# A conditioned fp32 block: the second entry's feed-forward weight in halves, its leaf sums on VectorE, and new places for late sums, last leaf sums and last stores

## The chip, the cores and the metric

The kernel runs on one core of one Trainium2 chip. The metric is the device time of one execution in microseconds. Five engines work side by side on the core: TensorE (PE, with its weight loads PEld), VectorE (DVE), ScalarE (ACT), GpSimd (POOL) and SyncE (SP, which issues most DMAs here; ACT issues some as well). Each engine runs its instructions in the order in which the program gives them; only semaphores tie engines together.

## The reference, cut to what matters

Input `x` has 2 batch entries of 2048 rows of 512 floats; `cond` has one row for each entry. All is fp32.

```python
emb = silu(t) @ ada_w + ada_b            # six rows of 512 for each entry
shift_msa, scale_msa, gate_msa, shift_mlp, scale_mlp, gate_mlp = split(emb, 6)
norm  = ln(x) * (1 + scale_msa) + shift_msa
h     = gelu(norm @ ssm_w1 + ssm_b1)               # 512 -> 512, exact gelu
x     = x + gate_msa * (h @ ssm_w2 + ssm_b2)       # 512 -> 512
norm2 = ln(x) * (1 + scale_mlp) + shift_mlp
hf    = gelu_tanh(norm2 @ ff_w1 + ff_b1)           # 512 -> 1024
x     = x + gate_mlp * (hf @ ff_w2 + ff_b2)        # 1024 -> 512
```

## The kernel before, in words

**Blocks.** The 4096 rows are cut into 8 blocks of 512 rows. Blocks 0 to 3 belong to the first entry, blocks 4 to 7 to the second. Each block goes through four stages, named in the trace by their tiles: `hA` (first hidden layer), `oA` (its residual), `hC` (feed-forward hidden layer), `oC` (feed-forward residual). A hand-written order interleaves the blocks: turn `i` of the main loop runs `hC` of block i, `oA` of block i+1, `oC` of block i, and `hA` of block i+2. TensorE goes through these stages without a break where it can.

**Fewer multiplications by sums.** No matrix product is done directly. `hA` and `oA` use seven half-size products (P1 to P7, in the order P1, P2, P6, P5, P7, P3, P4) in place of eight. These need sums of quarters of both operands beforehand, and the results are read out of PSUM and added by VectorE (lines 680, 728, 767, 770). `hC` uses 26 products from a list (`HK_P`) over 28 "registers" of the activation; 20 of these are made by a list of sums and differences (`HK_B`, line 806), on GpSimd for most blocks and on VectorE for block 7. VectorE and ScalarE read each product of `hC` out (lines 885 and 882). `oC` for blocks 1 to 7 (`residual_in_leaves`) runs P1, P5 and P6 plainly (line 717), with weights P5 and P6 that are sums of quarters, and cuts P2, P3 and P4 once more into seven "leaf" products each (line 750). The eight matmuls of the plain P7 are strewn between the first four leaves, two after each, so that TensorE has work while VectorE reads leaves. Both the activation's and the weight's leaves need sums of their own (line 340): `leaf_sums` gives `sums24` and `sums3` for the activation, `leaves_of_weight` eight sums for the weight (tile `fw_t`).

**The gate is folded into the weight.** Instead of multiplying the output by the gate, `weight_of_second` multiplies the weight `fw2` by it: eight multiplications on VectorE, one for each 128 rows (line 388), then four sums of quarters on GpSimd (tile `fw_s`, 128x1024). The gate differs between the entries, so the weight has to be loaded again and multiplied and summed again before `oC` of block 4. This is the list `fold`: eight multiplications, four sums, eight leaf sums. Before the change, the load (2 MB) is issued at the end of turn 3, the multiplications are hooked into `hC` of block 4 and `oA` of block 5, and all twelve sums stand on GpSimd at the end of `oA` of block 5, ahead of the norm's small scale instructions of that block (lines 501 to 519), which the program hooks into P1 of `oC`.

**Hooks.** Side work is put between products by `hook(hooks, places, ops)`: a place is the product after which the op is issued (a number in `hC`, a name such as P5 in the other stages). Within a place the order of the `hook` calls holds. In `residual_in_leaves`, `places` maps the leaf number r to a hook name.

**What the next norm needs.** In `oC` of block i the norm of block i+1 is made: statistics by VectorE (492, 493), scales by GpSimd (501 to 519), the normalised rows by ScalarE (532), a 32x32 transposition by VectorE (543), DMAs that finish it (552), the modulation by ScalarE (575; for block 7 half of it on VectorE, 577). In blocks up to 5 the transpositions of the rows 0 and 1 stand on VectorE between the reading of P5 and the reading of P6.

**The end.** Block 7 has no next block. Its `hC` sums, `sums24` and `sums3` run on VectorE between the last reading of `hC` and the first reading of `oC`. The finished rows are stored by SyncE in four DMAs (line 773): rows 0 and 2 of each group of four after leaf P3, rows 1 and 3 after leaf P4.

**PSUM.** Tiles are taken in rotation from pools of two buffers for each tag (`y`, `x`, `v`, `t`), so a product that takes a buffer waits until VectorE has read what was in it. The same holds within a stage where a second product is summed into a bank already read once.

Of the kernel before, what the change touches and what calls it, by code (L numbers as in the profile page):

```python
# [140 lines left out]
def kernel(  # L141
# [17 lines left out]
    P = 128  # L159
# [53 lines left out]
    def load_w(name, w, t=None, eng=nc.sync):  # L213
        if t is None:
            t = const.tile([P, w.shape[0] // P, w.shape[1]], F32, tag=name, name=name)
        eng.dma_start(out=t, in_=w.rearrange("(k p) n -> p k n", p=P))
        return t

    def load_row(t, row):
        nc.sync.dma_start(out=t, in_=row.unsqueeze(0).to_broadcast([P, D]))  # L220
# [480 lines left out]
    def residual_in_leaves(name, i, hops, wops, leaf_wops, kdim, hooks, last=False):  # L701
# [55 lines left out]
                )  # L757

        p7 = list(plain("P7"))
        places = {1: "P5", 3: "P7", 5: "P3", 6: "P4"}  # L760
        left = len(p7)
        for r, f in enumerate(LEAVES):
            t, e = LEAF_AT[f]
            for n in range(2):
                leaf("P23", n, f)
            d = xt[:, t, :].rearrange("p (q d) -> p q d", q=2)[:, :, e * P : (e + 1) * P]
            nc.vector.tensor_tensor(d, leaf_ps["P23", LEAF_BANK[f]][:, :2, :], d, ALU.add)
            leaf("P4", 0, f)
            d = xt[:, 2 + t, e * P : (e + 1) * P]
            nc.vector.tensor_tensor(d, leaf_ps["P4", LEAF_BANK[f]][:, 0, :], d, ALU.add)  # L770
            if last and f in ("P3", "P4"):
                for row in (t if f == "P4" else 0, 2 + t if f == "P4" else 2):
                    nc.sync.dma_start(out=out_blk[i][:, row, :], in_=xt[:, row, :])
            now, p7 = p7[: PLAIN_P7[r]], p7[PLAIN_P7[r] :]
            run(now)
            if now and not p7:
                read("P7", "22", "21")
            if r in places:
                hooked(places[r])

# [151 lines left out]
    def run(ops):  # L932
        for op in ops:
            op()
# [208 lines left out]
    fold = None  # L1143


    for i in range(1, NBLK):
# [18 lines left out]
            hook(hooks, (14, 16, 18, 20), [lambda c=c: n1[i + 2].turn(c) for c in range(C)])  # L1165
            hook(hooks, (20,), [n1[i + 2].move])
        if fold:
            hook(hooks, (2, 6, 23, 25), fold[:4])
        if (i + 1) % PER_B == 0 and nxt:
            hook(hooks, (0,), [lambda: load_gate(5, (i + 1) // PER_B)])  # L1170
        if (i + 2) % PER_B == 0 and nx2:
            hook(hooks, (0,), [lambda: load_gate(2, (i + 2) // PER_B)])
        hook(hooks, (20,), hC.summed(0, nc.gpsimd))
        hC.products(fa, fb[i], hooks, last or i == 1)

        hooks = {}
        hook(hooks, EARLY, hC.summed(1, nc.gpsimd if nxt else nc.vector))
        sums24, sums3 = hC.leaf_sums(*hC.leaf_room(nxt, nx2), nc.gpsimd if nxt else nc.vector)
        hook(hooks, ("P5",), sums24)
        if nxt:  # L1180

            if nx2:
                hook(hooks, ("P7",), n1[i + 2].moved())
            if fold:
                hook(hooks, EARLY, fold[4:8])
                hook(hooks, ("P7",), fold[8:])
            hook(hooks, ("P2", "P6"), [lambda p=p: seed(f"oC_{i}", gb[5], p) for p in range(2)])
            n2[i + 1] = Norm(i + 1, 2)
            hook(hooks, ("P3", "P4"), n2[i + 1].stats())
            residual(f"oA_{i + 1}", i + 1, hA[i + 1], w2_ops, KD // 2, hooks)  # L1190
        else:
            for p in EARLY:
                run(hooks.get(p, ()))
            run(sums3)
        fold = None

        hooks = {}
# [3 lines left out]
        if nxt:  # L1201

            hook(hooks, ("P1",), [lambda: n2[i + 1].scales(on_dve=not nx2)])
            hook(hooks, ("P1",), sums3)
            hook(hooks, ("P1",), [lambda c=c: n2[i + 1].normal(c) for c in range(C)])
            turns = ("P2", "P2", "P6") if nx2 else ("P1",)
            hook(hooks, turns, [lambda c=c: n2[i + 1].turn(c) for c in range(C)])
            hook(hooks, turns[-1:], [lambda: n2[i + 1].move((nc.sync, nc.scalar))])
# [40 lines left out]

        if refold5:  # L1250
            load_w("fw2", fw2, fw2_sb)
            take_gate(5, b)
            fw2_ops, fold = weight_of_second(fw2_sb, fw2_s, gate[5, b], (nc.vector,))
            leaf_wops, leaf_fold = leaves_of_weight(fw2_sb, fw2_s, nc.gpsimd)
            fold += leaf_fold
        hooks = {}
        if refold5:
            hook(hooks, ("P6",), [multiply_5])
        if refold2:
            take_gate(2, b)  # L1260
            w2_ops, w2_fold = weight_of_second(w2_sb, w2_s, gate[2, b], (nc.vector,))
# [48 lines left out]
```

## Time and profile before

| | us |
|---|---|
| median of 3 runs | 613.57 |
| lowest, highest | 613.17, 614.61 |
| the profiled execution's own time | 612.66 |
| its span, first to last instruction | 610.9 |

| engine | busy us | share of the span |
|---|---|---|
| PE | 585.6 | 96% |
| PEld | 515.3 | 84% |
| DVE | 401.2 | 66% |
| POOL | 385.1 | 63% |
| ACT | 234.1 | 38% |

The profile comes from one execution. The chain of work that ended last is 85% TensorE, 5% GpSimd, 5% VectorE, 2% ScalarE and 2% DMA. Times inside the trace are counted from the start of the span. An engine's name with a q (SPq, ACTq) is its queue of issued instructions; `PEclk` is the clock that TensorE was granted, 1.00 being full speed.

### The profile page before, as it was taken

The numbers are of one execution on the slowest core, as the hardware profiler recorded it, in microseconds if no ns is written. First come the engines' busy times: TensorE is split into PE (matmuls) and PEld (weight loads), VectorE is DVE, ScalarE is ACT, GpSimd is POOL, SyncE is SP. The second block draws the span as 40 slices with busy tenths as digits, with TensorE's granted clock in tenths as the row PEclk, the third lists the DMA queues.
The fourth block names the chain that finished last, engine by engine and source line by source line (L and its number), as shares of the span: only waits on it lengthen the run. The fifth ranks groups of instructions, "written<-read, shape, count | busy, mean of one in ns | idle before, by whom it ended". The sixth has DMA issues, their size and how long they took to land.

```text
span 610.9 us, 8959 instructions
## 1 busy us (share of the span) xinstructions
PE 585.6 (96%) x3127; PEld 515.3 (84%) x3127; DVE 401.2 (66%) x734; ACT 234.1 (38%) x396; POOL 385.1 (63%) x471
## 2 busy tenths in 40 slices
PE   7999999999999999999999999489999999997996
PEld 4888888888899888988899888388888988886876
DVE  4978889897565575767566587064756446569673
ACT  3234536216513472245533472042553336122510
POOL 2884549999964956489962959947686393720300
PEclk9999999999999999999999999879999999999999
DMA  8991233210514015320325313031030400031002
GB/s 321 396 353 27 63 69 96 79 69 0 139 38 120 0 40 185 70 87 0 85 77 162 109 24 115 0 70 69 1 70 1 138 2 1 1 70 69 2 0 70
DMA packets 23561, 50.18 MB, mean 82 GB/s; under 512 B 4528, under 2 KB 4572, under 8 KB 22620
## 3 DMA queue, kind: packets, MB, share of 16 engines
q1 hardware_dynamic: 20480, 45.38, 23.5%
q10 hardware_dynamic: 3036, 4.22, 2.9%
q8 instruction: 25, 0.41, 0.3%
q14 instruction: 20, 0.16, 0.1%
HBM read 26.51 MB, written 8.40 MB: 57 GB/s over the span
## 4 chain that ended last, share of the span: by engine, by line
PE 85%; POOL 5%; DVE 5%; ACT 2%; DMA 2%; issue 1%; SPq 0%; DVEq 0%; POOLq 0%; ACTq 0%
PE px_hC L868 10%; PE py_oC L717 9%; PE py_hA L458 9%; PE py_oA L458 8%; PE py_hC L868 7%; PE pv_hC L868 7%; PE pl_oC_P_y L750 6%; PE pv_hA L458 5%; PE pv_oA L458 4%; PE pl_oC_P_v L750 3%; PE py_hC L458 2%; PE px_hA L458 2%; PE pv_oC L717 2%; PE py_oC L458 2%; PE px_oA L458 2%; PE pl_oC_P_x L750 2%
## 5 line engine op out<-in xcount | busy, mean ns | idle before, releaser
L575 ACT ACTIVATE nT<-nT,mod,mod 128x512 f32<-128x512 f32 x54 | 39.6, 803 | 105.5 <-DMA nT<-blocks 87.4
L717 PE MATMUL py_oC<-fw,hClo 128*128 128x256 f32 x224 | 56.0, 389 | 11.6 <-DVE x L728 11.6
L532 ACT ACTIVATE nT<-x,nmr,rstd 128x512 f32<-128x512 f32 x56 | 42.4, 803 | 62.9 <-POOL nmr L519 46.6
L340 POOL TENSOR_TENSOR hSC<-hClo,hChi 128x512 f32<-128x512 f32 (+1 forms) x17 | 20.1, 1189 | 67.1 <-ACT hChi L863 51.8
L501 POOL TENSOR_SCALAR ve<-mv 128x4 f32<-128x4 f32 x16 | 3.7, 231 | 82.1 <-DVE mv L493 75.4
L717 PEld LDWEIGHTS py_oC<-fw,hClo 128*128 128x128 f32 x224 | 41.4, 195 | 16.5 <-DVE x L728 11.9
L492 DVE BATCH_NORM_STATS2 st<-x 128x6 f32<-128x512 f32 x64 | 43.4, 678 | 5.1 <-DMA x<-in_x_dram 4.8
L543 DVE STREAM_TRANSPOSE blocks<-nT 128x512 f32<-128x512 f32 x56 | 37.9, 694 | 13.3 <-ACT nT L532 13.0
L868 PE MATMUL py_hC<-forms,fw 128*128 128x256 f32 x168 | 40.8, 379 | 0.0
L885 DVE TENSOR_TENSOR hClo<-hClo,py_hC 128x512 f32<-128x512 f32 x42 | 28.4, 681 | 16.9 <-ACT hClo L882 10.3
L806 POOL TENSOR_TENSOR forms<-forms 128x256 f32<-128x256 f32 x48 | 35.7, 743 | 2.8
L868 PEld LDWEIGHTS py_hC<-forms,fw 128*128 128x128 f32 x168 | 31.8, 190 | 4.4
L680 DVE TENSOR_TENSOR x<-py_oA,x 128x512 f32<-128x512 f32 x32 | 22.1, 689 | 19.6 <-PE py_oA L458 15.2
L885 DVE TENSOR_TENSOR hChi<-hChi,pv_hC 128x512 f32<-128x512 f32 x35 | 23.3, 683 | 17.1 <-PE pv_hC L868 17.1
L458 PE MATMUL py_hA<-nT,w 128*128 128x256 f32 x128 | 30.4, 380 | 0.0
L868 PE MATMUL px_hC<-forms,fw 128*128 128x256 f32 x112 | 27.6, 379 | 0.0
L863 ACT ACTIVATE hClo<-hClo,colsT 128x256 f32<-128x256 f32 x56 | 25.3, 499 | 5.2 <-DVE hClo L885 4.7
L728 DVE TENSOR_TENSOR x<-py_oC,x 128x512 f32<-128x512 f32 x28 | 18.7, 687 | 12.9 <-PE py_oC L717 12.8
L717 PE MATMUL py_oC<-fw_s,hSC 128*128 128x256 f32 x112 | 25.4, 380 | 1.4 <-DVE x L728 1.4
L458 PE MATMUL py_oA<-w,hA 128*128 128x256 f32 x112 | 26.5, 379 | 0.0
L458 PEld LDWEIGHTS py_hA<-nT,w 128*128 128x128 f32 x128 | 23.7, 190 | 3.1 <-DVE hA L632 0.2
L806 POOL TENSOR_TENSOR forms<-nT,forms 128x256 f32<-128x256 f32 x36 | 25.8, 738 | 0.5
(292 smaller groups left out, 1572.4 us busy)
## 6 DMA issues: line engine op xcount, KB each, us to landing
nT<-blocks SPq DMA_DIRECT2D x168, 64.0 KB
x<-in_x_dram SPq DMA_DIRECT2D x7, 1024.0 KB
out_dram<-x SPq DMA_DIRECT2D x14, 512.0 KB
ada<-in_L_cond_ada_w_dram SPq DMA_DIRECT2D x6, 1024.0 KB
fw<-in_L_cond_ff_w_dram SPq DMA_DIRECT2D x3, 2048.0 KB
nT<-blocks ACTq DMA_DIRECT2D x56, 64.0 KB
w<-in_L_cond_ssm_w_dram SPq DMA_DIRECT2D x3, 1024.0 KB
x<-in_x_dram SPq DMA_DIRECT2D x2, 512.0 KB
```

Of the source, the lines that this page charges most:

```text
L458: nc.tensor.matmul(ps[b][j * apart][:, j, :], lhs(p, j, k), rhs(p, j, k), start=(fresh and j * (not apart) == 0 and k == 0), stop=(p in (" ...
L492: nc.vector.bn_stats(st, xs[self.i][:, c, :])
L532: nc.scalar.activation(t, x_c, AF.Identity, bias=self.nmr[:, c : c + 1], scale=self.rstd[:, c : c + 1])
L543: nc.vector.transpose(self.bl[:, :, :, c, :].rearrange("p m k q -> p k m q"), self.nT[:, c, :].rearrange("p (k m q) -> p k m q", k=KD, m=C),)
L575: nc.scalar.activation(dst, src, AF.Identity, bias=shift, scale=scale)
L680: nc.vector.tensor_tensor(d, ps[BANK[p]][:, js], d, ALU.add)
L717: yield lambda j=j, k=k: nc.tensor.matmul(ps[BANK[p]][:, j, :], hops(p, j, k), wops[p][:, k, :], start=False, stop=(k == kdim - 1), skip_g ...
L750: nc.tensor.matmul(t[:, n, :], hops.leaves["P4" if which == "P4" else ("P2", "P3")[n]][f][:, k, :], leaf_wops["P4" if which == "P4" else ( ...
L806: eng.tensor_tensor(reg[d], reg[a], reg[b], ALU.add if f == "+" else ALU.subtract)
L863: nc.scalar.activation(h, h, AF.Gelu_apprx_tanh, bias=fb1T[:, m : m + 1])
L868: nc.tensor.matmul(ps[b][:, j, :], fa[ra][:, j * P : (j + 1) * P], fb[rb].rearrange("p a (c q) -> p c a q", q=Q), start=(fresh and j == 0) ...
L885: nc.vector.tensor_tensor(dest(d), dest(d), ps[b], op)
```

## The change

Five things are edited.

1. **The second entry's `fw2`** is loaded in two halves of 1 MB. The first is issued inside `oC` of block 3, after the last plain P7 matmul; the second after that stage's matmuls, and ahead of the store of the block's second half of rows. The four multiplications of the first half are hooked into `hA` of block 5 (P5, P7, P3, P4), those of the second half into the first two products of `hC` of block 4. The four sums on GpSimd are hooked after product 5 of `hC` of block 4, ahead of the sums of `hC` itself. The eight leaf sums move from GpSimd to VectorE, hooked one or two at a place into `oA` of block 5.
2. **`HK_B` for block 7**: seven of the 20 sums stay in `oC` of block 6, three after leaf P7 (new hook `R4`), two after leaf P3, two after leaf P4. The other 13 stand between the products 0 to 4 of `hC` of block 7, and so between VectorE's readings of these products.
3. **The reading of plain P7** (line 728, two instructions) is issued after the readings of leaf P7 instead of before it, in every block from 1 to 7.
4. **`sums24` and `sums3` of the last block** run on GpSimd instead of VectorE; `sums3` of the other blocks is issued at P7 of `oA`, ahead of the norm's scales instead of after them.
5. **The last stores**: six DMAs instead of four, on SyncE and ScalarE in pairs. Rows 1 and 3 go in two pieces each, one after leaf P7 and one after leaf P4, both made of runs of 512 bytes.

```diff
+    def load_half(name, w, t, h):
+        K = t.shape[1] // 2
+        nc.sync.dma_start(
+            out=t[:, h * K : (h + 1) * K],
+            in_=w.rearrange("(h k p) n -> h p k n", h=2, p=P)[h],
+        )
...
-        places = {1: "P5", 3: "P7", 5: "P3", 6: "P4"}
-        left = len(p7)
+        places = {1: "P5", 3: "P7", 4: "R4", 5: "P3", 6: "P4"}
...
-            if last and f in ("P3", "P4"):
-                for row in (t if f == "P4" else 0, 2 + t if f == "P4" else 2):
-                    nc.sync.dma_start(out=out_blk[i][:, row, :], in_=xt[:, row, :])
+            if r == 4:
+                read("P7", "22", "21")
+            if last and r >= 4:
+                for eng, row in ((nc.sync, t), (nc.scalar, 2 + t)):
+                    if f == "P3":
+                        eng.dma_start(out=out_blk[i][:, row, :], in_=xt[:, row, :])
+                    else:
+                        cols = slice(e * P, (e + 1) * P)
+                        eng.dma_start(
+                            out=out_blk[i][:, row].rearrange("p (q d) -> p q d", q=2)[:, :, cols],
+                            in_=xt[:, row].rearrange("p (q d) -> p q d", q=2)[:, :, cols],
+                        )
             now, p7 = p7[: PLAIN_P7[r]], p7[PLAIN_P7[r] :]
             run(now)
-            if now and not p7:
-                read("P7", "22", "21")
...
         if fold:
-            hook(hooks, (2, 6, 23, 25), fold[:4])
+            hook(hooks, (0, 0, 1, 1), fold[:4])
+            hook(hooks, (5,), fold[4:8])
+        hook(hooks, (0, 0, 0, 0, 1, 1, 1, 2, 2, 3, 3, 4, 4), late_forms)
...
-        sums24, sums3 = hC.leaf_sums(*hC.leaf_room(nxt, nx2), nc.gpsimd if nxt else nc.vector)
+        sums24, sums3 = hC.leaf_sums(*hC.leaf_room(nxt, nx2), nc.gpsimd)
         hook(hooks, ("P5",), sums24)
+        hook(hooks, ("P7",), sums3)
...
-                hook(hooks, EARLY, fold[4:8])
-                hook(hooks, ("P7",), fold[8:])
+                hook(hooks, ("P1", "P2", "P6", "P5", "P5", "P7", "P7", "P3"), fold[8:])
...
-            run(sums3)
...
-            hook(hooks, ("P1",), sums3)
...
+            hook(hooks, ("P7",), [lambda: load_half("fw2", fw2, fw2_sb, 0)])
...
-                hook(hooks, ("P7",) * 9 + ("P3",) * 6 + ("P4",), [lambda n=n: late_form(n) for n in range(len(HK_B))])
...
+                late_forms = [lambda n=n: late_form(n) for n in range(len(HK_B))]
+                hook(hooks, ("R4",) * 3 + ("P3",) * 2 + ("P4",) * 2, late_forms[:7])
+                late_forms = late_forms[7:]
...
+        if refold5:
+            load_half("fw2", fw2, fw2_sb, 1)
         if not last:
             store(i, 1)
...
-            load_w("fw2", fw2, fw2_sb)
             take_gate(5, b)
...
-            leaf_wops, leaf_fold = leaves_of_weight(fw2_sb, fw2_s, nc.gpsimd)
+            leaf_wops, leaf_fold = leaves_of_weight(fw2_sb, fw2_s, nc.vector)
...
+            hook(hooks, ("P5", "P7", "P3", "P4"), fold[:4])
+            fold = fold[4:]
```

More of the change, by code (lines that the diff above doesn't have):

```diff
@@ L1142 @@
     store(0, 1)
-    fold = None
+    fold, late_forms = None, []
     for i in range(1, NBLK):
@@ L1174 @@
         hC.products(fa, fb[i], hooks, last or i == 1)
+        late_forms = []
         hooks = {}
         hook(hooks, EARLY, hC.summed(1, nc.gpsimd if nxt else nc.vector))
-        sums24, sums3 = hC.leaf_sums(*hC.leaf_room(nxt, nx2), nc.gpsimd if nxt else nc.vector)
+        sums24, sums3 = hC.leaf_sums(*hC.leaf_room(nxt, nx2), nc.gpsimd)
         hook(hooks, ("P5",), sums24)
+        hook(hooks, ("P7",), sums3)
         if nxt:
```

## The prediction

> **What bounds the kernel now.** The page comes first: TensorE is busy for 585.6 of 610.9 us and holds 85% of the chain that ended last. Only what makes TensorE wait, or run below its clock, can pay. So the next view is the list of waits of TensorE over the whole run (us in total, times, longest); its first two lines are what the change can reach.
>
> ```profile
> PE py_oC L717 <- DVE x L728: 12.9, 3, 10.7
> PE pl_oC_P_y L750 <- DVE x L767: 3.5, 1, 3.5
> ```
>
> The 12.9 are three waits: 10.68 in `oC` of block 4, 1.36 in `oC` of block 7, 0.87 in `oC` of block 6. The 3.5 is one, at the end of `oC` of block 6. The timeline of block 4 shows who made the longest (start, duration, engine, line, op; in brackets the idle time before it and its releaser):
>
> ```profile
> 375.72 2.38 POOL L340 TENSOR_TENSOR fw_s<-fw 128x1024 f32<-128x1024 f32 x1
> ...
> 385.12 1.27 POOL L340 TENSOR_TENSOR fw_t<-fw 128x512 f32<-128x512 f32 x1
> ...
> 393.09 0.23 POOL L501 TENSOR_SCALAR ve<-mv 128x4 f32<-128x4 f32 x1
> ...
> 396.19 2.93 ACT L532 ACTIVATE nT<-x,nmr,rstd 128x512 f32<-128x512 f32 x4 [18.23 <-POOL nmr L519]
> ...
> 398.37 0.65 DVE L728 TENSOR_TENSOR x<-py_oC,x 128x512 f32<-128x512 f32 x1
> 399.08 2.08 PE L717 MATMUL py_oC<-fw,hClo 128*128 128x256 f32 x4 [10.68 <-DVE x L728]
> ```
>
> VectorE's reading of P6 is late only because two transpositions (L543) stand before it, which wait for ScalarE, which waits for GpSimd's scales, which stand behind 17.4 us of weight sums (375.72 to 393.09). Block 3, which has no weight to make, starts the same scales at 309.98, 3.4 after its first `oC` matmul at 306.59; block 4 starts them 16.5 after its own at 376.54.
>
> The wait costs more than itself. In the windows the columns are the stretch, its length, busy time of PE, PEld, DVE, ACT and POOL, then PEclk, DMA share and GB/s:
>
> ```profile
> 388.00:399.00 11.00, 0.40 (x4) 0.21 (x2) 1.97 (x4) 2.81 (x4) 10.18 (x19) 0.65 0.00 0
> 399.00:402.00 3.00, 2.92 (x9) 2.56 (x10) 1.74 (x5) 0.12 (x1) 2.92 (x4) 0.50 0.18 40
> 402.00:405.00 3.00, 3.00 (x13) 2.73 (x12) 1.50 (x4) 0.00 (x0) 2.03 (x2) 0.51 0.62 143
> 405.00:408.00 3.00, 3.00 (x24) 2.87 (x24) 0.72 (x2) 0.00 (x0) 0.00 (x0) 1.00 0.76 172
> ```
>
> The clock falls during the wait and stays at half for 6 us after it. From the first `oC` matmul to the first `hA` matmul block 3 takes 329.88 - 306.59 = 23.29, block 4 takes 413.60 - 376.54 = 37.06. The excess, 13.77, is 10.68 of waiting and 3.09 of half clock.
>
> **Block 4, part by part.** GpSimd finishes block 5's `hA` sums at 354.22 and is then free. The four weight sums, 9.40 from 375.72 to 385.12, now follow there and end at 363.62. Everything behind them on GpSimd is pushed: eight `hC` sums and `sums24`, twelve of 1.26, end at 378.75, and `sums3` (2.86 in block 3) at 381.6. The products that need the `hC` sums start at 380.0 and 383.5, and the sums for them would end near 374, so that push is hidden by 6 us. Then come the scales (3.06), at 381.6 instead of 393.1. By block 3's pattern ScalarE gives row 1 some 1.6 later, two transpositions take 1.4, and the reading of P6 could begin at 387.7. TensorE needs it finished at 388.4. Without more, the wait would be about gone.
>
> More comes from the leaf sums, which go to VectorE while GpSimd is busy throughout. Lines from the start of the run show what two engines that both add SBUF to SBUF do to each other:
>
> ```profile
> 16.45 1.57 DVE L340 TENSOR_TENSOR nS<-nT,nS 128x512 f32<-128x512 f32 x1
> 17.44 1.72 POOL L340 TENSOR_TENSOR w<-w 128x512 f32<-128x512 f32 x1
> ```
>
> Alone these take 0.69 (block 7's sums on DVE) and 1.27. Over such pairs near 16 and 30 us VectorE's 512-wide sums take 0.80 to 1.65, mean 1.2, and GpSimd loses 0.4 for each; 256-wide pairs near 110 us give 0.83 to 0.95 on VectorE instead of 0.42 and about 0.2 lost on GpSimd. Eight leaf sums, four of each width, so delay GpSimd by 4 x 0.4 + 4 x 0.2 = 2.4 (bounds 0 and 3.5), and VectorE's share in `oA` grows to 4 x 1.2 + 4 x 0.87 = 8.3, where four multiplications of 0.68 stood. Laid out after each reading of 0.69, VectorE reaches P7's reading at 374.45 instead of 373.29 and ends it at 375.1; P4 reuses that bank and would start at 374.82: 0.3 lost (0 to 1.7, all sums at 1.65). The scales start at 384.0, P6 is read by 390.1, and P7, itself 0.45 later by then at 388.85, waits 1.3 (0 to 3.5).
>
> The Trainium skill's page "SBUF — State Buffer", section "Who interferes with whom", speaks against this edit: a VectorE instruction with two SBUF inputs and a GpSimd instruction that reads SBUF exclude each other for a whole instruction. By that rule the eight sums would cost GpSimd their full 4 x 0.69 + 4 x 0.42 = 4.4, and the wait would be 3.3; the rows above show about half of it, and I go by the rows.
>
> The multiplications cost nothing if the halves have landed. The first half may go once the plain P7 is through (325.9), ahead of SP's store that waits until 330.26. A 1 MB load beside the same sort of `nT` moves was issued at 372.13 and drained by 377, so this one is in near 332; the first multiplication stands at 337.7. Four of 0.68 go into gaps of 1.03 between `hA`'s readings and after the last of them. The second half follows the store at about 331; before, 2 MB issued at 331.2 drained by 342 (DMA share 0.26 in 340 to 342). It is wanted at 342.4, two multiplications fit before the reading at 343.99, and the other two replace one that stood at 345.20, pushing three readings by 0.7; product 8 waits for the third of them: 0.15 (0 to 0.7). Block 4 so gives 13.77 - 0.15 - 0.3 - 1.3 = **12.0**, bounds 8 and 13.8.
>
> **Late sums, block 6 into 7.** The 3.54 wait looks like a gain, but follow VectorE on:
>
> ```profile
> 550.59 1.29 DVE L728 TENSOR_TENSOR x<-py_oC,x 128x512 f32<-128x512 f32 x2 [0.57 <-PE py_oC L717]
> ...
> 564.52 0.68 DVE L885 TENSOR_TENSOR hChi<-hChi,px_hC 128x512 f32<-128x512 f32 x1
> ...
> 565.25 0.73 PEld L868 LDWEIGHTS px_hC<-forms,fw_s 128*128 128x128 f32 x4 [0.38 <-DVE hChi L885]
> ```
>
> VectorE runs without a gap for 14.6 us, and product 8 of `hC` waits for its end: it sums into the bank that product 5's reading (564.52) empties. After the change the same instructions, all 20 sums among them, still precede that reading. VectorE starts 0.56 sooner, with L577 before the P7 reading, and then waits 0.5 for leaf P7. TensorE trades one long wait for several short ones. Worth 0.1 (a loss of 0.8 to a gain of 0.8).
>
> **Last block.** Before the P6 wait of 1.36 VectorE does `sums24` and `sums3`, 584.50 to 588.58. On GpSimd, idle from 579.9, they end near 592 with the collisions; their first user, leaf P6, comes at 595.6. VectorE's own last three `hC` sums collide too and end at 586.3 instead of 584.6; P1 is then read by 587.0, P6 can start at 587.8. P6 was at 589.33 and took 3.69 instead of 3.45: gain 1.7 (1.2 to 1.8).
>
> **Reading of P7, `sums3` elsewhere: 0.** GpSimd has 4.18 idle before block 3's scales, `sums3` needs 2.86. The P7 reading would end near 328.9 there, the next `hA` needs its buffer at 329.88; if that cover failed, up to 0.2 in each of five blocks.
>
> **Last stores: loss 0.4.** The last 1 MB moves at full DMA share from 605.4 to 608.5 after issues from 604.55 on, so bytes set the end, not the issue. Now P7's two readings (1.29) come before the first store, which leaves 0.2 later. The trace's packet records have 512-byte packets (44) with a median of 27 ns and 2,048-byte ones at 84 to 92: four small for one large costs some 0.3 over 512 KB. Two issuing queues may hide 0.4 (bounds: gain 0.4, loss 1.2).
>
> **Sum.** 12.0 + 0.1 + 1.7 - 0.4 = 13.4. The profiled execution took 612.66 (span 610.9), so it would take 599.3; it lies 0.9 under the median, 613.57, which makes **600.2**.
>
> **Rivals.** *The late sums pay in full.* TensorE needs 1.3 + 8 x 0.86 from 553.2 to reach product 8, so it could gain up to 4: 596.3. For it: the waits name VectorE; against: its gapless 14.6 us. Chance 0.08. *Collision decides*: leaf sums at 1.65 and GpSimd 3.5 late; block 4 gives 8 to 9, time 603.5 to 604.5. The early rows speak for it. Chance 0.20. *The first half does not leave early*, because SP's wait covers later matmuls: it goes with the second near 330.5, `hA` of block 5 waits up to 3: 601 to 603. Chance 0.05. *Slower*: the multiplications in `hA` wait for a half still under way, and the readings queued behind them on VectorE stop TensorE. Each us after 337.7 costs one, and a long wait the 3.09 again; it decides from a landing at 348, and one at 352 would give 614 + 4 = 618. The drained 2 MB by 342 speak against it. Chance 0.02.
>
> **How the numbers follow.** My case has 0.63, no visible change 0.02. The range takes in the late sums' gain and most of the collision: 596.5 to 604.0. About 0.2% (1.2 us) is what a measurement can tell from no change: faster 0.96, same 0.02, slower 0.02.
>
> **What would show it.** In the profile after: scales (L501) of block 4 near 384; P7's wait there 1 to 2 instead of 10.7; PEclk 1.00 throughout 388 to 408; leaf sums (`fw_t`) on DVE at 0.9 to 1.6; no wait of 3.5 before leaf P4 of block 6 but product 8 of block 7's `hC` still gated by L885; no L728 wait in block 7. I am wrong if the multiplications (L388) show idle time before them on DMA, or if TensorE stands in `oA` of block 5.

## The result and the profile after

The changed kernel takes 597.44 us (median of 4 runs, 597.23 to 598.97) against 614.09 for the kernel before, run beside it (4 runs): ratio 0.9735, 95% interval 0.9713 to 0.9758. 600.2 was predicted, with a range of 596.5 to 604.0. The profiled execution took 597.23 us with a span of 595.4; against 612.66 and 610.9 that is 15.4 us less, where the prediction's sum was 13.4. (By these two medians it is 16.7 less: the profiled execution of the kernel before lies 1.4 under that kernel's median, the changed one 0.2 under its own.) The gains by place below are taken between the two profiles.

Lines of the changed kernel carry new numbers: the plain matmuls of `oC` are L724 (were 717), their readings L735 (728), the leaves L757 (750), the matmuls of `hC` L881 (868), their readings L898 and L895 (885, 882), the sums L347 (340), the sums for `hC` L819 (806), the norm's scales L508 to L526 (501 to 519).

The page of the changed kernel, its line of busy times and its line of granted clocks:

```profile
PE 582.9 (98%) x3127; PEld 512.5 (86%) x3127; DVE 405.9 (68%) x734; ACT 234.3 (39%) x396; POOL 388.8 (65%) x471
PEclk9999999999999999999999999999999999999999
```

TensorE is busy for 98% of the span instead of 96%. Its list of waits (us in total, times, longest):

```profile
PE px_hC L881 <- DVE hChi L898: 1.5, 1, 1.5
...
PE py_oC L724 <- DVE x L735: 1.2, 1, 1.2
PE py_hC L881 <- DVE forms L819: 0.9, 1, 0.9
PE px_hC L881 <- DVE forms L819: 0.5, 1, 0.5
```

The reading of `oC` by VectorE, 12.9 us in three waits before, is one wait of 1.2, in block 4. The 3.5 before leaf P4 of block 6 is gone; in its place stand three waits in `hC` of block 7 (0.9, 0.5 and 1.5 at products 0, 3 and 8).

The most useful reading is a table by stage: the time from the first matmul of a stage to the first matmul of the next, taken from TensorE's timeline (for the last stage, up to the end of the span). Times of whole runs scatter by 1 to 2 us in a place that nothing here edits: up to the first matmul of `oC` of block 0 the profiled executions of all kernels took 108.0 to 110.1 us. So effects below 2 us are read from the stages. "hC4" is `hC` of block 4.

| kernel | hC4 | oA5 | oC4 | oC6 | hC7 | oC7 to end | span |
|---|---|---|---|---|---|---|---|
| before | 22.49 | 12.09 | 37.06 | 28.13 | 22.69 | 29.97 | 610.9 |
| changed | 22.79 | 12.49 | 24.65 | 24.24 | 25.02 | 27.74 | 595.4 |
| 1. weight part undone | 22.49 | 12.09 | 39.54 | 24.24 | 25.02 | 27.99 | 609.9 |
| 2. leaf sums on GpSimd | 22.80 | 12.09 | 32.10 | 24.24 | 25.03 | 27.77 | 602.8 |
| 3. no leaf sums | 22.79 | 12.09 | 23.19 | 24.24 | 25.02 | 27.75 | 593.4 |
| 4. one load | 22.80 | 13.47 | 23.19 | 24.24 | 25.02 | 27.97 | 599.5 |
| 5. late sums back | 22.79 | 12.56 | 24.66 | 25.30 | 23.89 | 27.75 | 595.3 |
| 6. `sums3` behind the scales | 22.80 | 12.57 | 23.25 | 25.38 | 25.02 | 27.73 | 595.1 |
| 7. P7 read first | 22.79 | 13.47 | 23.52 | 24.15 | 25.03 | 27.03 | 595.0 |
| 8. last sums on VectorE | 22.79 | 12.56 | 24.66 | 24.24 | 25.02 | 29.31 | 598.4 |
| 9. four stores | 22.79 | 12.53 | 24.67 | 24.24 | 25.02 | 28.88 | 598.4 |
| 10. six stores, one queue | 22.79 | 12.51 | 24.67 | 24.24 | 25.02 | 27.75 | 595.9 |
| 11. 13 late sums on GpSimd | 22.79 | 12.54 | 24.67 | 24.25 | 24.50 | 27.73 | 595.0 |
| 12. three steps more | 22.49 | 12.85 | 23.25 | 24.24 | 24.50 | 27.75 | 594.1 |

The gain by place: block 4 lost 0.30 in `hC`, 0.40 in `oA`, and won 12.41 in `oC`, together **11.7**; blocks 6 and 7 won (28.13 + 22.69) - (24.24 + 25.02) = **1.56**; the last stage won 2.23, of which **1.60** up to VectorE's last instruction and **0.63** behind it (4.69 to 4.06); `oC` of blocks 1 to 3 won 0.1 each, **0.3**; the start was 0.35 longer. The sum is 15.4.

**Block 4.** The timeline of the changed kernel there:

```profile
354.54 2.38 POOL L347 TENSOR_TENSOR fw_s<-fw 128x1024 f32<-128x1024 f32 x1
...
373.34 1.49 DVE L347 TENSOR_TENSOR fw_t<-fw_s 128x256 f32<-128x256 f32 x1
...
384.38 0.23 POOL L508 TENSOR_SCALAR ve<-mv 128x4 f32<-128x4 f32 x1
...
389.67 0.65 DVE L735 TENSOR_TENSOR x<-py_oC,x 128x512 f32<-128x512 f32 x1
...
390.38 1.13 PE L724 MATMUL py_oC<-fw,hClo 128*128 128x256 f32 x4 [1.20 <-DVE x L735]
```

The weight sums start at 354.5 instead of 375.7, the scales at 384.4 (predicted 384.0), P6 is read by 390.3 (predicted 390.1) and P7 waits 1.20 (predicted 1.3). The windows over that wait and behind it (stretch, length, busy PE, PEld, DVE, ACT, POOL, then PEclk, DMA share, GB/s) show that the half clock is gone as well:

```profile
388.00:391.00 3.00, 1.80 (x14) 1.56 (x13) 2.68 (x5) 2.41 (x4) 2.92 (x3) 1.00 0.00 0
391.00:394.00 3.00, 3.00 (x24) 2.85 (x23) 2.53 (x7) 0.00 (x0) 1.71 (x2) 1.00 0.40 87
```

### The profile page after: what moved, and what is told of

It is laid out like the page before. It is cut to its first block, busy times and chain, and to the rows that moved or that the text cites. A ratio compares the mean times of both kernels' runs of the same rounds, so it can differ in the third digit from the quotient of the medians.

```text
span 595.4 us, 8969 instructions
## 1 busy us (share of the span) xinstructions
PE 582.9 (98%) x3127; PEld 512.5 (86%) x3127; DVE 405.9 (68%) x734; ACT 234.3 (39%) x396; POOL 388.8 (65%) x471
## 4 chain that ended last, share of the span: by engine, by line
PE 85%; DVE 4%; POOL 4%; DMA 2%; issue 2%; SPq 1%; ACT 1%; DVEq 0%; POOLq 0%
PE py_oC L724 11%; PE px_hC L881 9%; PE py_hA L465 9%; PE py_hC L881 7%; PE pv_hC L881 7%; PE py_oA L465 7%; PE pl_oC_P_y L757 6%; PE pv_hA L465 4%; PE pv_oA L465 3%; PE pv_oC L724 3%; PE pl_oC_P_v L757 3%; PE px_hA L465 2%; PE py_oC L465 2%; PE py_hC L465 2%; PE px_oA L465 2%
## 5 line engine op out<-in xcount | busy, mean ns | idle before, releaser
L347 POOL TENSOR_TENSOR hSC<-hClo,hChi 128x512 f32<-128x512 f32 (+1 forms) x17 | 20.6, 1216 | 61.4 <-ACT hChi L876 47.6
L724 PE MATMUL py_oC<-fw,hClo 128*128 128x256 f32 x224 | 54.2, 380 | 1.2 <-DVE x L735 1.2
L508 POOL TENSOR_SCALAR ve<-mv 128x4 f32<-128x4 f32 x16 | 3.7, 231 | 77.0 <-DVE mv L500 70.2
L724 PEld LDWEIGHTS py_oC<-fw,hClo 128*128 128x128 f32 x224 | 40.4, 190 | 5.7 <-DVE x L735 1.4
L881 PE MATMUL py_hC<-forms,fw 128*128 128x256 f32 x168 | 40.8, 379 | 0.0
L898 DVE TENSOR_TENSOR hClo<-hClo,py_hC 128x512 f32<-128x512 f32 x42 | 28.4, 680 | 16.6 <-ACT hClo L895 10.2
L819 POOL TENSOR_TENSOR forms<-forms 128x256 f32<-128x256 f32 x48 | 35.6, 742 | 2.8
L881 PEld LDWEIGHTS py_hC<-forms,fw 128*128 128x128 f32 x168 | 31.8, 190 | 4.4
L898 DVE TENSOR_TENSOR hChi<-hChi,pv_hC 128x512 f32<-128x512 f32 x35 | 23.3, 683 | 14.7 <-PE pv_hC L881 14.7
L881 PE MATMUL px_hC<-forms,fw 128*128 128x256 f32 x112 | 27.8, 380 | 0.5 <-DVE forms L819 0.5
L819 POOL TENSOR_TENSOR forms<-nT,forms 128x256 f32<-128x256 f32 x36 | 25.8, 739 | 0.5
L876 ACT ACTIVATE hChi<-hChi,colsT 128x256 f32<-128x256 f32 x56 | 25.1, 496 | 1.9 <-DVE hChi L898 1.9
L895 ACT ACTIVATE hClo<-px_hC 128x512 f32<-128x512 f32 x21 | 12.5, 597 | 33.7 <-PE px_hC L881 27.9
```

Source lines behind the costliest of these rows:

```text
L724: yield lambda j=j, k=k: nc.tensor.matmul(ps[BANK[p]][:, j, :], hops(p, j, k), wops[p][:, k, :], start=False, stop=(k == kdim - 1), skip_g ...
L819: eng.tensor_tensor(reg[d], reg[a], reg[b], ALU.add if f == "+" else ALU.subtract)
L876: nc.scalar.activation(h, h, AF.Gelu_apprx_tanh, bias=fb1T[:, m : m + 1])
L881: nc.tensor.matmul(ps[b][:, j, :], fa[ra][:, j * P : (j + 1) * P], fb[rb].rearrange("p a (c q) -> p c a q", q=Q), start=(fresh and j == 0) ...
L898: nc.vector.tensor_tensor(dest(d), dest(d), ps[b], op)
```

## The experiments

Each kernel is the changed kernel with the edit shown. The theory: block 4's chain (weight sums, scales, reading of P6) carries nearly all of the gain, and collisions of VectorE's leaf sums with GpSimd's sums set what is left of the wait; the late sums are worth nothing. The first rivals: the late sums pay; the collisions are free; the early first half is not needed.

**1. The weight part undone.**

```diff
-            hook(hooks, (0, 0, 1, 1), fold[:4])
-            hook(hooks, (5,), fold[4:8])
+            hook(hooks, (2, 6, 23, 25), fold[:4])
...
-                hook(hooks, ("P1", "P2", "P6", "P5", "P5", "P7", "P7", "P3"), fold[8:])
+                hook(hooks, EARLY, fold[4:8])
+                hook(hooks, ("P7",), fold[8:])
...
-            hook(hooks, ("P7",), [lambda: load_half("fw2", fw2, fw2_sb, 0)])
...
-            load_half("fw2", fw2, fw2_sb, 1)
...
+            load_w("fw2", fw2, fw2_sb)
...
-            leaf_wops, leaf_fold = leaves_of_weight(fw2_sb, fw2_s, nc.vector)
+            leaf_wops, leaf_fold = leaves_of_weight(fw2_sb, fw2_s, nc.gpsimd)
...
-            hook(hooks, ("P5", "P7", "P3", "P4"), fold[:4])
-            fold = fold[4:]
```

> The changed kernel with the whole of part 1 undone: the second entry's ff weight is loaded in one piece after block 3, multiplied and summed where it was before, leaf sums on GpSimd; all other parts stay. My theory: part 1 is worth 12 to 13 of the 15.4 us between the two profiles, and with sums3 now ahead of the scales the old queue on GpSimd is 2.9 longer still, so block 4 loses 14 to 16: 611 to 614, with a wait of 12 to 14 us of TensorE on L735 in oC of block 4 and the clock at half after it. Rival, that the gain is spread over the other parts: 600 to 606.

Measured: 611.47 us, ratio to before 0.9962 (0.9948 to 0.9975). Its list of waits:

```profile
PE py_oC L724 <- DVE x L735: 12.4, 1, 12.4
...
PE pv_oC L724 <- POOL fw_s L347: 0.9, 1, 0.9
```

`oC` of block 4 takes 39.54, more than the 37.06 of before: with the old weight path, `sums3` ahead of the weight sums and the scales makes the wait longer. The weight sums start at 378.68 instead of 375.72, and P5 now waits 0.9 for the first of them. All other stages keep their gain. So the weight part is 14 us of the changed kernel's time.

**2. The eight leaf sums back on GpSimd,** at the places where VectorE now has them.

```diff
-            leaf_wops, leaf_fold = leaves_of_weight(fw2_sb, fw2_s, nc.vector)
+            leaf_wops, leaf_fold = leaves_of_weight(fw2_sb, fw2_s, nc.gpsimd)
```

> The changed kernel with only the eight leaf sums of the weight back on GpSimd, at the same places. My theory: GpSimd then reaches the scales of block 5 about 5 us later (7.9 of its own sums more, 2.5 of collisions less), near 389.5; the wait of TensorE in oC of block 4 grows from 1.2 to 6 or 7, long enough for the clock to fall: 602 to 606. Rival, that the earlier four big sums were enough and the move to VectorE only brings collisions: 596 to 598, wait under 2.

Measured: 604.54 us (603.86 to 604.86), ratio 0.9849 (0.9823 to 0.9875). The list of waits:

```profile
PE py_oC L724 <- DVE x L735: 6.9, 1, 6.9
```

and two windows, the second one after TensorE has gone on at 395.93:

```profile
391.00:394.00 3.00, 0.00 (x0) 0.00 (x0) 0.12 (x1) 0.97 (x2) 2.33 (x8) 0.79 0.00 0
...
397.00:400.00 3.00, 3.00 (x16) 2.82 (x15) 0.84 (x4) 0.00 (x0) 1.26 (x2) 0.57 0.52 118
```

The stage is 32.10 - 23.19 = 8.9 longer than without the wait: 6.9 of waiting and 2.0 more, most of it half clock. (A wait without half clock also costs a little more than itself: the 1.20 in the changed kernel makes this stage 24.65 - 23.19 = 1.46 longer.) Of the 12.41 won in this stage, the earlier load and the four earlier quarter sums are worth 37.06 - 32.10 = 5.0; the move of the leaf sums to VectorE is worth the other 7.5, less 0.4 in `oA`.

**3. The leaf sums left out.**

```diff
-                hook(hooks, ("P1", "P2", "P6", "P5", "P5", "P7", "P7", "P3"), fold[8:])
+                del fold[8:]
```

> The changed kernel without the eight leaf sums of the second entry's weight (left out: blocks 4 to 7 use the leaf sums of the first entry's weight). Nothing else is moved. My theory: what block 4 still loses against block 3 (0.3 in hC, 0.4 in oA, 1.46 in oC by the stage starts) is, but for the 0.3 in hC, collisions of these sums with GpSimd's: GpSimd's twelve 512-wide sums in oA of block 5 go back to 1.27 from 1.3 to 1.7, the scales start near 381.5 instead of 384.4, oA takes 12.09 and oC about 23.2 to 23.4: 1.6 to 1.9 faster than the changed kernel, 595.6. Rival, that GpSimd is late because of its longer queue alone (sums3 ahead of the scales, 2.9): the scales start at 383.9 or later, oC still takes 24.0 or more, at most 0.9 faster.

Measured: 595.19 us (595.12 to 596.51), ratio 0.9706 (0.9679 to 0.9732). One of GpSimd's sums and the scales in its timeline:

```profile
367.63 1.27 POOL L347 TENSOR_TENSOR hSC<-hChi,hSC 128x512 f32<-128x512 f32 x1
...
381.92 0.23 POOL L508 TENSOR_SCALAR ve<-mv 128x4 f32<-128x4 f32 x1
```

The same sum in the changed kernel, where VectorE adds beside it:

```profile
367.79 1.73 POOL L347 TENSOR_TENSOR hSC<-hChi,hSC 128x512 f32<-128x512 f32 x1
```

With nothing on VectorE that adds SBUF to SBUF, GpSimd gets to the scales at 381.92 instead of 384.38. Its run of sums began 0.15 earlier here (363.81 against 363.96), so the sums on VectorE delay GpSimd by 2.3 us. All of that lies in the eight of its sums that take 1.33 to 1.73 in the changed kernel and 1.26 to 1.28 here. `oA` of block 5 is back at 12.09 and `oC` of block 4 at 23.19, so the eight sums cost TensorE 0.40 + 1.46. (How much of the 0.40 VectorE's own work would cost without collisions was not separated.) The prediction had 2.4 for GpSimd; the rule of the Trainium skill ("SBUF — State Buffer", "Who interferes with whom"), taken as a full exclusion for all eight sums, gave an estimate of 4.4. The measured 2.3 agrees with the rows of before and not with that estimate.

**4. One load of 2 MB at the old place,** all else as changed.

```diff
-            hook(hooks, ("P7",), [lambda: load_half("fw2", fw2, fw2_sb, 0)])
...
-            load_half("fw2", fw2, fw2_sb, 1)
...
+            load_w("fw2", fw2, fw2_sb)
```

> The changed kernel with the ff weight loaded in one 2 MB piece after block 3's oC, as before, while the multiplications stay in hA of block 5 and the first products of hC of block 4. My theory: VectorE's first multiplication at 337.9 waits until the whole piece has landed, near 341.5, and hA's readings behind it wait too: TensorE loses 2.5 to 4 in hA of block 5, about 600.5, and L395 shows some 3.5 of idle time before it on DMA. Rival, that the halves are not needed because the load lands in time: within 0.5 of the changed kernel.

Measured: 601.35 us (601.06 to 601.41), ratio 0.9798 (0.9778 to 0.9818). The first multiplication on VectorE:

```profile
343.14 0.69 DVE L395 TENSOR_TENSOR fw<-fw,pgate 128x512 f32<-128x512 f32 x1 [3.76 <-DMA fw<-in_L_cond_ff_w_dram]
```

`hA` of block 5 takes 15.05 instead of 12.09. The early half carries 3.0 us there: without it, VectorE stands on the load and TensorE behind it. The stages `oA` of block 5 and `oC` of block 4 take 0.98 more and 1.46 less, so the net is 2.5; another 1.4 of the longer span lies ahead of `oC` of block 0, in the start. This comes close to the rival "the first half does not leave early" (there the halves leave together near 330.5, ahead of the second store and not behind it), and its price, up to 3 in `hA`, was right.

**5. The late sums back in `oC` of block 6.**

```diff
-                hook(hooks, ("R4",) * 3 + ("P3",) * 2 + ("P4",) * 2, late_forms[:7])
-                late_forms = late_forms[7:]
+                hook(hooks, ("P7",) * 9 + ("P3",) * 6 + ("P4",), late_forms)
+                late_forms = []
```

> The changed kernel with the 20 late sums of block 7 back in oC of block 6 (nine after leaf P5's hook P7, six, five). My theory: the 3.5 us wait at leaf P4 of block 6 comes back, the waits in hC of block 7 (2.9 together) go, since product 8 needs all 20 sums and five readings from VectorE either way: 0 to 0.8 slower than the changed kernel, 597.4 to 598.3. Rival, that moving the late sums gave the 1.6 us that blocks 6 and 7 gained: 599.0. Second rival, that the whole 3.5 was saved: 601.

Measured: 597.42 us (597.05 to 600.36), ratio 0.9745 (0.9713 to 0.9776). The list of waits:

```profile
PE pl_oC_P_y L757 <- DVE x L773: 1.8, 1, 1.8
...
PE px_hC L881 <- DVE hChi L898: 0.8, 1, 0.8
```

Part of the wait moves from `hC` of block 7 into `oC` of block 6 (1.8 comes back of the 3.5, and 0.8 stays at product 8, where none was expected), and the two stages together take 49.2, as in the changed kernel (49.3). The move of the late sums is worth nothing: VectorE has the same work in front of product 8 either way.

**6. `sums3` behind the scales again,** in all blocks but the last.

```diff
-        hook(hooks, ("P7",), sums3)
+        if not nxt:
+            hook(hooks, ("P7",), sums3)
...
+            hook(hooks, ("P1",), sums3)
```

> The changed kernel with sums3 of blocks 1 to 6 behind the scales again, as before the change (the last block's stay on GpSimd). My theory: in block 4 the scales start 2.9 us earlier, near 381.5, and TensorE's wait of 1.2 there goes; in block 6 the scale instructions on VectorE (L516, L518, L519), 0.16 each in the changed kernel, take 0.6 to 0.7 again beside sums3 on GpSimd, and the 0.9 us wait on L735 comes back together with a later start of VectorE's late sums. Net 0.5 faster to 0.7 slower than the changed kernel: 596.9 to 598.1. Rival, that the late sums alone made the gain in blocks 6 and 7: block 6 does not move, 596.2.

Measured: 597.08 us (596.90 to 597.36), ratio 0.973 (0.9704 to 0.9755). The total hides two effects of opposite sign. `oC` of block 4 wins 1.40, since the scales no longer stand behind `sums3`. `oC` of block 6 loses 1.14, and a wait of 0.9 on L735 is there again. The reason is in VectorE's timeline of block 6. There four of the norm's scale instructions run on VectorE. Kernel before (`sums3` on GpSimd beside them):

```profile
534.84 0.68 DVE L509 TENSOR_TENSOR e<-r,ve 128x4 f32<-128x4 f32 x1 [0.35 <-POOL r L503]
...
536.36 0.65 DVE L512 SCALAR_TENSOR_TENSOR nmr<-mv,rstd 128x4 f32<-128x4 f32 x1
```

Changed kernel (`sums3` already done):

```profile
523.21 0.16 DVE L516 TENSOR_TENSOR e<-r,ve 128x4 f32<-128x4 f32 x1 [0.35 <-POOL r L510]
...
523.80 0.16 DVE L519 SCALAR_TENSOR_TENSOR nmr<-mv,rstd 128x4 f32<-128x4 f32 x1
```

This experiment:

```profile
521.75 0.68 DVE L516 TENSOR_TENSOR e<-r,ve 128x4 f32<-128x4 f32 x1 [0.36 <-POOL r L510]
...
523.27 0.65 DVE L519 SCALAR_TENSOR_TENSOR nmr<-mv,rstd 128x4 f32<-128x4 f32 x1
```

Three of the four instructions, on four elements each, take 0.58 to 0.68 instead of 0.16 when GpSimd's sums run beside them. They stand in the chain to P6's reading: their last one ends 6.94 after the first matmul of the stage instead of 5.51. These 1.4 us make a wait of 0.9 at TensorE and a stage that is 1.14 longer. That is the cause of 1.14 of the 1.56 which blocks 6 and 7 won.

**7. The reading of plain P7 first again.**

```diff
-            if r == 4:
-                read("P7", "22", "21")
...
+            if now and not p7:
+                read("P7", "22", "21")
```

> Only the reading of plain P7 stands before the readings of leaf P7 again, in every block from 1 to 7. Of the 1.56 us that blocks 6 and 7 won between the first matmul of oC of block 6 and that of oC of block 7, the run with sums3 behind the scales took back 1.14; the order of these two readings is what is left for the other 0.4. My theory: 0.2 to 0.5 us slower than the changed kernel (597.6 to 597.9), in oC of block 6 and in the tail, where rows 2 and 3 then leave with P7's reading in front of the first store of all; the stages oC of blocks 1 to 4 stay as they are. Rival: the order is worth nothing anywhere, 597.4 +- 0.2, and the 0.4 comes from L584 alone. Rival: it frees P7's buffer sooner for the next hA in every block and the kernel gets faster by up to 0.5, 596.9.

Measured: 597.26 us (596.53 to 598.27), ratio 0.9725 (0.9705 to 0.9745), so no difference in total, and the theory failed in its places. `oC` of block 6 does not get longer (24.15 against 24.24); `oC` of blocks 1 to 3 gets 0.09 longer each, which is their gain; and the last stage gets 0.7 shorter. In block 4 the collisions fall differently: `oA` of block 5 takes 1.0 more, `oC` of block 4 1.1 less. What the other 0.4 of blocks 6 and 7 is due to stays open: undone one at a time, the late sums, this order and `sums3` give back 0, 0 and 1.14, and the effect of two together was not run.

The last stores explain the 0.7. SyncE's and ScalarE's queues, changed kernel:

```profile
588.42 0.38 SPq L785 DMA_DIRECT2D out_dram<-x  x1
...
589.93 0.41 ACTq L785 DMA_DIRECT2D out_dram<-x  x1
```

and experiment 7, where P7 is read before the leaf:

```profile
588.96 0.38 SPq L783 DMA_DIRECT2D out_dram<-x  x1
...
589.16 0.42 ACTq L783 DMA_DIRECT2D out_dram<-x  x1
```

P7's reading writes rows 2 and 3 only. In the changed kernel row 1's piece therefore leaves at once, but row 3's waits for the two P7 readings behind the leaf. The windows (same columns as above) of the changed kernel show the DMA engines idle in between:

```profile
589.39:589.89 0.50, 0.50 (x6) 0.50 (x6) 0.50 (x2) 0.00 (x0) 0.00 (x0) 1.00 0.84 240
589.89:590.39 0.50, 0.50 (x7) 0.50 (x6) 0.50 (x3) 0.00 (x0) 0.00 (x0) 1.00 0.00 0
590.39:590.89 0.50, 0.50 (x6) 0.48 (x5) 0.28 (x2) 0.00 (x0) 0.00 (x0) 1.00 0.02 6
```

In experiment 7 they are full from 590.12 on without a gap:

```profile
590.12:590.62 0.50, 0.50 (x7) 0.50 (x6) 0.16 (x1) 0.00 (x0) 0.00 (x0) 1.00 1.07 289
```

**8. The last block's `sums24` and `sums3` back on VectorE.**

```diff
-        sums24, sums3 = hC.leaf_sums(*hC.leaf_room(nxt, nx2), nc.gpsimd)
+        sums24, sums3 = hC.leaf_sums(*hC.leaf_room(nxt, nx2), nc.gpsimd if nxt else nc.vector)
```

> Only sums24 and sums3 of block 7 go back from GpSimd to VectorE. My theory: the wait of P6 for VectorE's reading of P1 (L735) in oC of block 7 is back with 1.2 to 1.5 us and that stage takes 29.2 to 29.5 us instead of 27.71 to the end of the span; 1.6 us slower than the changed kernel, 599.0. Rival (the collisions with GpSimd's hC sums cost VectorE as much as the moved sums did): no difference, 597.4.

Measured: 600.24 us (598.90 to 600.39), ratio 0.9768 (0.9749 to 0.9787). The last stage is 1.57 longer, and P6 waits:

```profile
577.42 3.69 PE L724 MATMUL py_oC<-fw_s,hSC 128*128 128x256 f32 x16 [1.30 <-DVE x L735]
```

The rest of the difference in whole time lies in the start (109.6 us up to `oC` of block 0 against 108.3). In the changed kernel the collisions are there too, and P6 is early enough all the same:

```profile
570.04 1.75 DVE L347 TENSOR_TENSOR hClo<-hClo 128x512 f32<-128x512 f32 x1
...
574.61 3.62 PE L724 MATMUL py_oC<-fw_s,hSC 128*128 128x256 f32 x16
```

**9. The four stores of before,** after the changed order of readings.

```diff
-            if last and r >= 4:
-                for eng, row in ((nc.sync, t), (nc.scalar, 2 + t)):
...
+            if last and f in ("P3", "P4"):
+                for row in (t if f == "P4" else 0, 2 + t if f == "P4" else 2):
+                    nc.sync.dma_start(out=out_blk[i][:, row, :], in_=xt[:, row, :])
```

> The changed kernel with the four last stores of before (rows 0 and 2 after leaf P3, rows 1 and 3 after leaf P4, all on SP). My theory after the first comparison: from VectorE's last instruction to the end the changed kernel takes 4.06, the kernel before 4.69, because row 1's first piece leaves 3 us before the last reading; with the old stores it takes 4.6 to 4.8 again: 0.5 to 0.8 slower than the changed kernel, about 598. Rival, my prediction: pieces of 512 bytes cost more than the earlier start brings, 0.4 faster, 597.

Measured: 598.78 us (598.11 to 600.20), ratio 0.976 (0.9735 to 0.9785); the last stage is 1.14 longer. The direction was expected, but not the size: from VectorE's last instruction to the end it takes 5.20, where 4.6 to 4.8 was expected.

**10. Six stores, all issued by SyncE.**

```diff
-                for eng, row in ((nc.sync, t), (nc.scalar, 2 + t)):
+                for eng, row in ((nc.sync, t), (nc.sync, 2 + t)):
```

> The changed kernel with all six last stores issued by SP, none by ScalarE. If the second issuing queue makes the gain at the end: from VectorE's last instruction to the end 4.4 to 4.8 instead of 4.06. If the earlier first piece does: 4.0 to 4.3, since the last two issues lie only 0.3 to 0.4 apart and the transfers are still draining then.

Measured: 597.38 us (597.02 to 598.93), ratio 0.9739 (0.9715 to 0.9763); the last stage is as in the changed kernel (27.75 against 27.74). The second queue does nothing. That agrees with the Trainium skill ("DMA: Bandwidth & Descriptors", "Issuing engines are not separate DMA queues"), by which a second issuing engine saves only the time to issue.

With experiments 7 and 9 the end can be split. From the end of VectorE's last instruction to the end of the span, in us:

| | P7 read first | P7 read after the leaf |
|---|---|---|
| four stores | 4.69 (before) | 5.20 (experiment 9) |
| six stores | 3.34 (experiment 7) | 4.06 (changed) |

Six stores win 1.1 to 1.35; the order of the readings takes 0.5 to 0.7 of it back.

**11. The 13 sums of block 7's `hC` on GpSimd.** GpSimd has nothing to do from 523 to 561 us, and VectorE's stretch of work sets product 8.

```diff
-                        late["ops"] = form(nc.vector)
+                        fb[i + 1] = n2[i + 1].registers()
+                        late["ops"] = sums_of_registers(
+                            HK_B, fb[i + 1], (nc.vector,) * 7 + (nc.gpsimd,) * 13
+                        )
```

> The changed kernel with one more step: the last 13 of the 20 sums for block 7's hC go from VectorE to GpSimd, which is idle from 523 to 561 us. VectorE's gapless stretch of 14.7 us before product 8 loses 13 sums of about 0.38, 4.9 us. My theory (the stretch sets product 8): the wait of 1.48 us at product 8 is gone, hC of block 7 takes 22.9 to 23.5 us instead of 25.02, 1.5 to 2.1 us faster than the changed kernel, 595.3 to 595.9. Rival: GpSimd needs 0.72 for each of these sums (577.27 in the profile of the changed kernel), 9.4 us from about 543.8, so they end at 553.2, and products 3 to 7 wait for them as long as product 8 waited for VectorE: no difference, 597.4, with waits of L881 on GpSimd's L819. Rival: collisions with VectorE's readings make it slower, 598 to 599.

Measured: 596.86 us (596.66 to 598.53), ratio 0.9723 (0.9703 to 0.9743); `hC` of block 7 takes 24.50 instead of 25.02. In its timeline:

```profile
544.10 3.20 POOL L819 TENSOR_TENSOR forms<-forms 128x256 f32<-128x256 f32 x4 [20.80 <-DVE forms L819]
...
547.36 1.13 PE L881 MATMUL px_hC<-forms,fw 128*128 128x256 f32 x4 [1.68 <-POOL forms L819]
```

Product 8 no longer waits, as the theory had it; but product 3 now waits 1.68 instead of 0.48 for the first four sums, 0.80 each on GpSimd against 0.45 on VectorE (1.79 for the same four). The rival was right about the mechanism; of the gain of 1.5 to 2.1 that the theory expected, 0.5 came. Leaving these four on VectorE is the next step; it was not run.

**12. Three steps more:** experiment 11, `sums3` behind the scales in block 4 alone, and the fourth multiplication two products later.

```diff
-            hook(hooks, (0, 0, 1, 1), fold[:4])
+            hook(hooks, (0, 0, 1, 3), fold[:4])
...
-        hook(hooks, ("P7",), sums3)
+        sums3_late = bool(fold)
+        if not sums3_late:
+            hook(hooks, ("P7",), sums3)
...
+            if sums3_late:
+                hook(hooks, ("P1",), sums3)
```

> The changed kernel with three steps more: the 13 late sums on GpSimd as in the run beside this one; in block 4 alone, sums3 behind the norm's scales again (worth 1.40 us in oC of block 4 where it was done for all blocks); and the last of the second half's four multiplications hooked after product 3 of block 4's hC instead of product 1, so that three readings of VectorE are not pushed (hC of block 4 took 22.79 us where it took 22.49 before: up to 0.3). If the three add up: 597.4 - 1.7 - 1.4 - 0.2 = 594.1, range 593.4 to 594.8. If the run beside this one shows no gain: 595.8.

Measured: 595.75 us (595.35 to 596.71), ratio 0.9702 (0.9683 to 0.9720). That is 1.7 less than the changed kernel by the medians, which were taken at different times; the intervals of the two ratios to before overlap a little (0.9683 to 0.9720, 0.9713 to 0.9758). The stages say it more sharply: the steps add up to `hC` of block 4 22.49 (0.30 won), `oC` of block 4 23.25 (1.40 won), `hC` of block 7 24.50 (0.52 won); `oA` of block 5 gives 0.36 back. Together 1.86 less than the changed kernel. The expected 593.4 to 594.8 was missed, mainly because the step of experiment 11 was counted at 1.7 and is worth 0.5.

## Why the prediction was right, and where it was off

**The bound and the place were right.** The long wait was GpSimd's queue ahead of the scales, and it went. By the parts of the sum:

| step | predicted | measured |
|---|---|---|
| block 4 | 12.0 | 11.7 |
| late sums, blocks 6 and 7 | 0.1 | 0 by the move (experiment 5); these stages won 1.56 |
| last block | 1.7 | 1.6 |
| order of readings, `sums3` elsewhere | 0 | 0.3 in blocks 1 to 3 (experiment 7), and 1.14 of the 1.56 (experiment 6) |
| last stores | -0.4 | 0.6 |

**Block 4** came out step by step: the quarter sums on GpSimd from 354.5, the scales within 0.4 of the time given (the weight sums had begun 0.3 later than the 354.22 assumed), the wait within 0.1, the loss in `oA` 0.40 for 0.3, the multiplications 0.30 for 0.15. The collisions in the early rows of the trace were a good price list as a sum: 2.3 for 2.4 on GpSimd, 8.4 for 8.3 on VectorE. As single prices they were not: 512-wide sums took VectorE 0.81 to 0.97 (mean 1.2 was assumed), 256-wide ones 0.89 to 1.49 (0.87 was assumed). That these two errors cancel is luck. One of the signs of being wrong that the prediction names did appear, TensorE standing in `oA` of block 5; its own sum had 0.3 there.

**Off, first: `sums3` ahead of the scales was costed at nothing outside block 4.** The step looked only at GpSimd's idle time in front of the scales. It left out that in block 6 VectorE runs four of the scale instructions itself, beside `sums3`, and that 0.68 and 0.65 for four elements stood in the trace of before, next to a 0.16. This is 1.14 us (experiment 6). In block 4 the same move costs 1.40, which the prediction had counted as part of the push on the scales.

**Off, second: the sign of the last stores.** Two terms were wrong. "P7's two readings (1.29) come before the first store" holds for row 3 and not for row 1, which P7 does not write; and "bytes set the end, not the issue" left out that the DMA engines were idle until the first issue at 604.55, so pieces that leave earlier take bytes out of the end: their issues come 3.0 and 1.5 us before VectorE's last instruction ends in the changed kernel, 2.7 and 2.5 before it in experiment 7. The order of readings does cost, 0.5 to 0.7 rather than 0.2; the earlier pieces win 1.1 to 1.35 rather than nothing. The price of the packet size was right: the DMA share, summed over the windows of the tail, is 3.45 us against 3.22 before, 0.24 more for 0.3 assumed, but it lies in front of an end that comes sooner. The two queues, which might have hidden 0.4, hide nothing (experiment 10). The term's own two prices, 0.2 and 0.3, add up to 0.5 rather than the 0.4 that went into the sum.

**The remaining distance.** The errors of the terms add up to 2.0 (0.63 + 0.4 for the stores, 1.46 in blocks 6 and 7, 0.3 in blocks 1 to 3, less 0.35 in the start, 0.3 in block 4 and 0.1 in the last block), which is 15.4 - 13.4. The predicted time is near the measured one because block 4 was 12 of the 13.4 and was right; the other terms were small, and two of them were wrong.

**The rivals.** "The late sums pay in full" is out: experiment 5 moves the wait and no time. "Collision decides" has the right mechanism at a price far too high: with block 4 at 8 to 9, it lets the sums cost 13.77 - 0.15 less 8 to 9, which is 4.6 to 5.6; they cost 1.9 (experiment 3). "The first half does not leave early" did not happen. SyncE's queue issued it at 326.12, ahead of the store, and its price without the early issue is 3.0 in `hA` of block 5 (experiment 4). "Slower" needed a landing after 348; even the single late load lets VectorE go on at 343.14.

## What to carry to other kernels

When an engine's queue delays a small instruction that others wait for, move the bulk ahead of it into that engine's idle time, and price the two-engine collisions that follow by rows of the same trace in which the same two engines add at once. Look for those collisions at tiny instructions too: an instruction on four elements that takes 0.65 in one place and 0.16 in another is a sign, and reordering the other engine's work by a few us removes it. Compare variants by stage rather than by whole time when the expected effects are smaller than the scatter of a stage that no edit touches; and undo the parts one by one, since a total of no difference (experiments 6 and 7) can hide a gain and a loss.

## What was not expected of the hardware

- Three of four VectorE instructions on 128x4 elements took 0.58 to 0.68 us beside GpSimd's 256-wide sums and 0.16 without them, a factor of four; a 512-wide sum took up to 1.75 instead of 0.69.
- The collisions cost GpSimd 2.3 us for eight sums of VectorE, and they change with small shifts: with P7 read first, the same eight sums took 0.68 to 1.78 in another pattern, and the loss moved from `oC` of block 4 into `oA` of block 5 with the same total (37.0 against 37.1).
- A wait of TensorE of 10.7 us cost 3.1 more than itself, one of 6.9 cost 2.0 more, most of it half clock. One of 3.54, at the end of `oC` of block 6 in the kernel before, brought no half clock: the granted clock stays at 1.00 in all windows from 548 to 563 us. The stage there is 4.94 over 23.19 for waits of 3.54 and 0.87, 0.26 more for each, as with the short wait of 1.20. The Trainium skill ("TensorE: Matmul & The Clock Gate", "What's actually happening") gives a window of about 3.4 us that runs freely. The granted clock in these traces agrees with it: it fell 2.9 us into the wait of 10.7 (at 391.28), 3.7 into that of 6.9 (experiment 2, at 392.75) and 4.0 into that of 12.4 (experiment 1, at 393.62), and the half clock lasted 13.65, 6.83 and 13.65 us, that is 4, 2 and 4 times 3.41. As it fell after 2.9 in one case, the 3.54 that passed without a drop is no safe length.
